# Row transposes of maxima and the masked sums issued as products of 32 columns, and placed behind the values of their step

## The chip, the cores and the metric

The kernel runs on one core of a Trainium2 chip. The metric is the device time of one execution in microseconds (us). Five engines take part, each with its own queue of instructions: TensorE (PE; its weight loads are listed apart as PEld), VectorE (DVE), ScalarE (ACT), GpSimd (POOL) and SyncE (SP), which issues most transfers. They meet through semaphores.

## The reference

One decoder layer over four sequences of 512 tokens with 512 features and 16 heads of 32. Biases, layer norms and the gate's softmax are as usual; cut to what matters:

```python
# self attention: causal softmax, masked scores are -inf
scores = jnp.where(causal, (q @ k.T) * SCALE, -jnp.inf)
x = x + softmax(scores) @ v @ o_w.T + o_b
# cross attention on ctx, without projections: masked scores are -10000, so in the first
# rows the masked keys can weigh as well
scores = jnp.where(causal, (qh @ kh.T) / sqrt(hd), -10000.0)
x = x + softmax(scores) @ vh
# feed forward: shared relu MLP, plus the expert output weighted by the top-2 gate
h = layernorm(x)
x = x + relu(h @ W_up.T) @ W_down.T + rw.sum() * (h @ W_expert)
```

## The kernel before

The work of a sequence (a "batch", 0 to 3) is laid out with features on the 128 partitions: four groups `g` of four heads of 32 features each, and 512 tokens along the free dimension, in four blocks of 128. Each attention has two passes.

`with_maxima` (line 905) computes scores with queries on partitions, and DVE takes the largest of each row. `split` (341) writes the negated maxima of a group as three bf16 parts into `parts[g % 2]`. `rows` (352) turns them on PE: four transposes of 128 by 128, one a token block, with `identb`, into a PSUM tile named `mt_...`, which is then copied to `mrow[g]`.

`attend` (954) computes the scores again with keys on partitions, in ten steps `n`. `scores` (393) makes the four heads' products with 32 rows of the array each (line 405) and adds the negated maxima as further products with `mrow[g]` (416). They fill two PSUM pairs, `sc_..._0` and `sc_..._1`, two heads in each. ACT takes the exponential of each pair (439), POOL zeroes the part above the diagonal (447), and `values`, called with two steps' delay, multiplies by the values (482), four heads side by side in 32 columns of the array each. The sums of exponentials are partly added up on DVE first (`add_up`, 547 to 552) and multiplied with ones afterwards (`summed`, 558).

In the cross attention masked keys can count, so there is more. `masked_sums` (371) spreads a group's maxima over its heads with one product of 128 columns by 512 (`same`, 374), `masked` (377) takes the exponential on ACT (381) as `ct_...`, and its closure `weigh` (385 to 389) is a memset and two multiplications of 128x512 on DVE. For groups 0 and 1 this is in the first pass; for groups 2 and 3 it is in `attend`. `divide(g)` (588) adds the weighted sums to the PSUM results and inverts the denominator: two additions that read `pv_...` from PSUM (592, 593), a 32x32 block transpose, a reciprocal and a transpose back (579, 581, 582). `scale` (571, 574) multiplies the group with it, on POOL for groups 0 to 2 and on DVE for group 3. For group 1 `divide` is called in the `values` of step 6; for groups 2 and 3, in the two `values` after the loop. `add_cross` (751) then transposes all four groups of the result, group by group, with PE (756).

PSUM holds four pairs of banks. The order on PE, DVE, ACT and POOL is the order in which the Python code issues (`manual_schedule`): each of these engines works through its queue as written, and an instruction that waits holds those behind it. The code that the change moves stands in the loop of `attend`:

```python
for n, pieces in enumerate(units):
    waiting.append(a.scores(pieces))
    if n in late:
        ...
        copies += a.rows(late[n], both)
        more = [a.masked_sums(2, both)] if two else []
        ...
    if a.cross and n == 7:
        todo.append(a.masked(*a.masked_sums(3)))
    if n in (4 if a.joined is None else 6, 6, 9) and todo:
        todo.pop(0)()
    if n in (3, 4) and put_off:
        put_off.pop(0)()
    if len(waiting) > 2:
        values()
```

`late` names the groups whose maxima are turned inside `attend`: groups 2 and 3 at step 3 of a self attention, group 3 at step 3 of the cross attentions 0 to 2, groups 2 and 3 at steps 3 and 5 of cross attention 3. `todo` holds the closures `weigh` of groups 2 and 3: they come at steps 6 and 9.

Of the kernel before, what the change touches and what calls it, by code (L numbers as in the profile page):

```python
# [18 lines left out]
P = 128  # L19
# [7 lines left out]
def decoder_layer(  # L27
# [21 lines left out]
    nc = tc.nc  # L49
    B, S, D = x.shape  # L50
    NH = 16
    HD = D // NH
    NT = S // P
    NC = D // P
    HG = P // HD
# [9 lines left out]
    def pair(name):  # L65

        return ps.tile([P, 2, S], F32, tag="ps", name=name)
# [65 lines left out]
    identb = const.tile([P, P], BF16, name="identb")  # L133
# [6 lines left out]
    same = const.tile([P, P], BF16, name="same")  # L140
# [34 lines left out]
    parts = []  # L175
# [90 lines left out]
    class Attention:  # L266
# [82 lines left out]
            nc.vector.tensor_copy(pt[:, :, :, 1], rest)  # L349
            nc.vector.tensor_tensor(pt[:, :, :, 2], rest, pt[:, :, :, 1], ALU.subtract)  # L350

        def rows(self, g, both=None, half=0):


            if both is None:
                tp = ps.tile([P, NT, P], BF16, tag="ps", name=f"mt_{self.name}_{g}")
            else:
                bank = both[:, 0, :].bitcast(BF16)
                tp = bank[:, half * S : (half + 1) * S].rearrange("p (i q) -> p i q", q=P)
            for i in range(NT):  # L360
                nc.tensor.transpose(tp[:, i, :], parts[g % 2][:, i, :], identb)
            self.mrow[g] = work.tile(
                [P, S], BF16, tag="mrow", name=f"mrow_{self.name}_{g}", bufs=4
            )

            def copy(engine=nc.vector.tensor_copy):
                engine(self.mrow[g], tp.rearrange("p i q -> p (i q)"))

            return [copy]

        def masked_sums(self, g, both=None):

            bc = (pair(f"mb_{self.name}_{g}") if both is None else both)[:, 1, :]
            nc.tensor.matmul(bc, lhsT=same, rhs=self.mrow[g], start=True, stop=True)
            return g, bc

        def masked(self, g, bc):
# [527 lines left out]
    def with_maxima(steps, a, first=0, norms=()):  # L905


        norms = list(norms)
        run(steps[:first])
        fill = matmuls(steps[first:])  # L910
        total = sum(1 if step.__name__ in ("share", "gate") else NC for step in steps[first:])

        units = []
        for g in range(0, NC, 2):
            units += [[(g, 1), (g + 1, 1)]]
            units += [u for k in (g, g + 1) for u in ([(k, 2), (k, 0)], [(k, NT - 1)])]

        lead = 2 if first else 0
        for _ in range(lead):
            next(fill)  # L920
        done, due, jobs, late = lead, float(lead), [], {3: NC - 1}
        todo = []
        for n, pieces in enumerate(units):
            new = a.maxima(pieces)
            if todo:
                todo.pop()(nc.gpsimd)
            if norms and n % 2 == 0:
                new.append(norms.pop(0))
            due += (total - lead) / len(units)

            count = round(due) - done
            for k in range(count):
                next(fill, None)
                done += 1
                if k == min(1, count - 1) and n in (5, 7):
                    jobs = a.rows((n - 5) // 2) + jobs
                if k == min(1, count - 1) and a.cross and n in (6, 8):
                    todo.append(a.masked(*a.masked_sums((n - 6) // 2)))
                if n == len(units) - 1 and k == count - (2 if count > 4 else 1):
                    if total >= 2 * len(units):  # L940
                        if a.cross:
                            a.rows(2)[0](nc.scalar.copy)
                    else:
                        late = {3: 2, 5: NC - 1}
                run(jobs[:1])
                jobs = jobs[1:]
            run(jobs)
            jobs = new
        for _ in fill:
            pass  # L950
        run(jobs)
        return late

    def attend(a, late):


        units = []
        for g in range(0, NC, 2):
            units += [[(g, 0)], [(g, 3), (g, 1)], [(g, 2), (g + 1, 2)]]
            units += [[(g + 1, 0)], [(g + 1, 3), (g + 1, 1)]]  # L960
        waiting, held, todo = [], [], []

        def values():
            made = waiting.pop(0)
            a.values(made)

            if len(made) > 1 and made[0][1] == 2:
                held.append(made[1:])
            elif waiting and waiting[0][0][1] > 0:
                if made[0][1] == 0 and held:  # L970
                    a.add_up(held.pop())
                a.add_up(waiting[0] if waiting[0][0][1] == 3 else waiting[0][:1])
                if waiting[0][0][1] == 2 and waiting[0][1][0] == a.joined:
                    a.join(waiting[0][1], waiting[1][0])

        for n, pieces in enumerate(units):
            waiting.append(a.scores(pieces))
            if n in late:
                two = a.cross and late[n] == NC - 1
                together = not a.cross and len(late) == 1  # L980
                both = pair(f"mt_{a.name}_both") if two or together else None
                copies = a.rows(2, both, 1) if together else []
                copies += a.rows(late[n], both)

                more = [a.masked_sums(2, both)] if two else []
                for copy in copies:
                    copy(nc.scalar.copy)
                todo.extend(a.masked(*each) for each in more)
            if a.cross and n == 7:
                todo.append(a.masked(*a.masked_sums(3)))  # L990
            if n in (4 if a.joined is None else 6, 6, 9) and todo:
                todo.pop(0)()
            if n in (3, 4) and put_off:
                put_off.pop(0)()
            if len(waiting) > 2:
                values()
        while waiting:
            values()

    with tc.manual_schedule(engines=BY_HAND):  # L1000
# [11 lines left out]
        for b in range(B):  # L1012
            more = b + 1 < B
# [4 lines left out]
            late = with_maxima(between_self, sa, skip, norms)  # L1018
            if b == B - 1:
                e.x = load_x(b)  # L1020
            attend(sa, late)
            if b > 0:
                add_bias(e)
# [8 lines left out]
            late = with_maxima(steps[3:], ca)  # L1032
            if b + 2 < B:
                after.x = load_x(b + 1)
            attend(ca, late)
            if more:
                cvs[b + 1] = load_cv(b + 1)
# [74 lines left out]
```

## Time and profile before

| | |
|---|---|
| median of 3 runs | 804.1 us (803.87 to 805.67) |
| span of the profiled execution | 803.7 us, 0.4 us under that median |
| mean granted TensorE clock | 0.998 |
| busy: PE, DVE, ACT, POOL | 794.0, 565.9, 395.2, 339.6 us |
| PE instructions (matrix products, weight loads) | 5588, 5592 |

A span runs from the first instruction to the last. Products on PE are pipelined: the profile's duration of one is longer than the time after which the next may start, so durations on PE overlap, and the times of start say more. A float32 product that is not a transpose stands in the trace as two records.

### The profile page before, as it was taken

What the parts mean: (1) busy time and instruction counts of PE and PEld (TensorE: products, weight loads), DVE (VectorE), ACT (ScalarE), POOL (GpSimd) and SP (SyncE); (2) the same over time, 40 slices, a digit from 0 to 9 for tenths busy, and PEclk for the clock granted to TensorE, in tenths of its full rate; (3) what the DMA queues carried; (4) which work ended last, traced back from release to release, by engine and by line L of the source; (5) the groups of instructions that cost most, each with busy time, mean ns of one, the idle gap of its engine ahead of it and who ended that gap; (6) DMA issues with size and microseconds to landing.
All of it is one profiled execution on the core that took longest, in us unless ns stands there. A gap on an engine that the chain in (4) does not pass through costs nothing.

```text
span 803.7 us, 13927 instructions
## 1 busy us (share of the span) xinstructions
PE 794.0 (99%) x5588; PEld 378.9 (47%) x5592; DVE 565.9 (70%) x963; ACT 395.2 (49%) x448; POOL 339.6 (42%) x523
## 2 busy tenths in 40 slices
PE   8999999999999999999999999999999999999998
PEld 6444454444444454444544455444444444444544
DVE  2378855889679854678867786588959766988512
ACT  2457516871456615567055742687156833674110
POOL 3434612564234732257332482256423652475100
PEclk9999999999999999999999999999999999999999
DMA  9710000001010000021100000000102000000101
GB/s 301 275 28 1 2 1 1 2 27 54 1 27 2 2 0 1 2 78 55 53 14 14 1 2 0 1 1 2 53 28 80 2 1 1 1 2 1 53 1 52
DMA packets 15282, 24.51 MB, mean 30 GB/s; under 512 B 2033, under 2 KB 5361, under 8 KB 15217
## 3 DMA queue, kind: packets, MB, share of 16 engines
q1 hardware_dynamic: 14496, 22.96, 8.6%
q8 instruction: 44, 0.72, 0.4%
q10 hardware_dynamic: 720, 0.66, 0.2%
q14 instruction: 22, 0.17, 0.1%
HBM read 19.42 MB, written 4.19 MB: 29 GB/s over the span
## 4 chain that ended last, share of the span: by engine, by line
PE 95%; ACT 2%; issue 1%; DMA 1%; DVE 0%; ACTq 0%
PE pm_qk L241 14%; PE pm_d L229 7%; PE pm_u L241 7%; PE pm_v L229 7%; PE pm_o L725 7%; PE pm_e L229 7%; PE pv_c L482 6%; PE pv_s L482 6%; PE sm_c L293 6%; PE sm_s L293 6%; PE sc_s L405 5%; PE sc_c L405 5%; PE sc_s L416 1%; PE sc_c L416 1%; PE tp_a L255 1%
## 5 line engine op out<-in xcount | busy, mean ns | idle before, releaser
L324 DVE TENSOR_REDUCE nm_s<-s_s 128x2 f32<-128x1024 f32 (+3 forms) x128 | 96.9, 810 | 34.7 <-POOL s_s L312 34.7
L324 DVE TENSOR_REDUCE nm_c<-s_c 128x2 f32<-128x1024 f32 (+3 forms) x128 | 95.8, 810 | 31.0 <-POOL s_c L312 31.0
L304 ACT COPY s_s<-sm_s 128x1024 f32<-128x1024 f32 x80 | 77.1, 1015 | 70.7 <-PE sm_s L293 36.7
L304 ACT COPY s_c<-sm_c 128x1024 f32<-128x1024 f32 x80 | 77.1, 1016 | 35.9 <-PE sm_c L293 16.2
L312 POOL TENSOR_SCALAR_AFFINE_SELECT s_c<-s_c 128x512 f32<-128x512 f32 (+1 forms) x80 | 43.9, 550 | 100.4 <-ACT s_c L304 100.4
L312 POOL TENSOR_SCALAR_AFFINE_SELECT s_s<-s_s 128x512 f32<-128x512 f32 (+1 forms) x80 | 43.8, 551 | 94.4 <-ACT s_s L304 94.4
L552 DVE TENSOR_TENSOR sum_s<-sum_s,pt_s 128x256 f32<-128x256 f32 (+2 forms) x72 | 59.9, 897 | 15.4 <-PE pv_s L482 15.4
L439 ACT ACTIVATE pt_c<-sc_c 128x1024 f32<-128x1024 f32 x64 | 61.7, 1031 | 18.1 <-PE sc_c L416 10.1
L447 POOL TENSOR_SCALAR_AFFINE_SELECT pt_c<-pt_c 128x512 f32<-128x512 f32 (+1 forms) x64 | 52.9, 833 | 20.7 <-ACT pt_c L439 20.2
L229 PE MATMUL pm_d<-wdown_sb,hT 128*128 128x512 f32 x128 | 61.5, 611 | 0.0
L241 PE MATMUL pm_qk<-xnT,wk_sb 128*128 128x512 f32 x128 | 61.0, 606 | 0.0
L241 PE MATMUL pm_u<-fT,wup_sb 128*128 128x512 f32 x128 | 59.3, 605 | 0.0
L439 ACT ACTIVATE pt_s<-sc_s 128x1024 f32<-128x1024 f32 x56 | 53.9, 1030 | 10.5 <-POOL pt_s L447 5.5
L229 PE MATMUL pm_v<-wv_sb,xnT 128*128 128x512 f32 x128 | 58.8, 600 | 0.0
L725 PE MATMUL pm_o<-wo_sb,oT_s 128*128 128x512 f32 x128 | 57.8, 596 | 0.0
L405 PE MATMUL sc_c<-cqT,ckT 32*128 32x384 f32 (+3 forms) x512 | 56.4, 464 | 0.9 <-ACT sum_c L439 0.9
L241 PE MATMUL pm_qk<-xnT,wq_sb 128*128 128x512 f32 x120 | 56.7, 605 | 0.0
L229 PE MATMUL pm_e<-wexp_sb,fT 128*128 128x512 f32 x120 | 56.3, 604 | 0.0
L447 POOL TENSOR_SCALAR_AFFINE_SELECT pt_s<-pt_s 128x512 f32<-128x512 f32 (+1 forms) x56 | 48.0, 865 | 16.9 <-ACT pt_s L439 16.2
L405 PE MATMUL sc_s<-qT,kT 32*128 32x128 f32 (+3 forms) x512 | 54.1, 464 | 0.9 <-ACT sum_s L439 0.9
L293 PE MATMUL sm_c<-ckT,cqT 32*128 32x512 f32 (+3 forms) x512 | 47.5, 460 | 0.0
L293 PE MATMUL sm_s<-kT,qT 32*128 32x512 f32 (+3 forms) x512 | 47.0, 461 | 0.0
(171 smaller groups left out, 1268.1 us busy)
## 6 DMA issues: line engine op xcount, KB each, us to landing
cv<-in_ctx_dram SPq DMA_DIRECT2D x16, 256.0 KB, 4.4
out_dram<-x SPq DMA_DIRECT2D x15, 256.0 KB, 2.0
xin<-in_x_dram SPq DMA_DIRECT2D x12, 256.0 KB, 2.8
x<-in_x_dram SPq DMA_DIRECT2D x12, 256.0 KB, 4.2
wq_sb<-in_wq_dram SPq DMA_DIRECT2D x2, 512.0 KB, 6.7
wk_sb<-in_wk_dram SPq DMA_DIRECT2D x2, 512.0 KB, 7.7
wv_sb<-in_wv_dram SPq DMA_DIRECT2D x1, 1024.0 KB, 7.8
wo_sb<-in_wo_dram SPq DMA_DIRECT2D x1, 1024.0 KB, 9.5
```

What stands on the lines that cost most here:

```text
L229: nc.tensor.matmul(pm, lhsT=lhs_t[:, c, t * P : (t + 1) * P], rhs=w[:, c, :], start=(c == 0), stop=(c == NC - 1),)
L241: nc.tensor.matmul(pm, lhsT=w[:, c, f * P : (f + 1) * P], rhs=rhs_t[:, c, :], start=(c == 0), stop=(c == NC - 1),)
L293: nc.tensor.matmul(scs[r // 2][:, r % 2, c : c + (i + 1) * P], lhsT=self.q_t[h, g, i * P : (i + 1) * P], rhs=self.k_t[h, g, : (i + 1) * P] ...
L304: nc.scalar.copy(s, scs[n])
L312: nc.gpsimd.affine_select(out=diagonal, in_=diagonal, compare_op=ALU.is_ge, fill=NEG, base=0, pattern=[[0, 2], [0, len(pieces)], [-1, P]], ...
L324: nc.vector.tensor_reduce(self.nm[g][:, i, 2 * n : 2 * n + 2], made[n][:, :, c : c + (i + 1) * P], axis=AX.X, op=ALU.max, negate=True,)
L405: nc.tensor.matmul(scs[r // 2][:, r % 2, c : c + S - j * P], lhsT=self.k_t[h, g, j * P : (j + 1) * P], rhs=self.q_t[h, g, j * P :], start= ...
L439: nc.scalar.activation(pt, scs[n], AF.Exp)
L447: nc.gpsimd.affine_select(out=diagonal, in_=diagonal, compare_op=ALU.is_ge, fill=0.0, base=0, pattern=[[0, 2], [0, len(pieces)], [1, P]], ...
L482: nc.tensor.matmul(pv[r * HD : (r + 1) * HD, u, j * P :], lhsT=ones if u else self.v[:, j, h * HD : (h + 1) * HD], rhs=pts[r // 2][:, r % ...
L552: nc.vector.tensor_tensor(to, to, pts[n][:, :, c : c + S - j * P], ALU.add)
L725: nc.tensor.matmul(pms[t // 2][:, t % 2, :], lhsT=a.out[:, c, t * P : (t + 1) * P], rhs=wo_sb[:, c, :], start=(c == 0), stop=(c == NC - 1),)
```

## The change

`rows` and `masked_sums` get an argument `columns`, which the calls in `attend` set. With it each transpose of 128 by 128 becomes four plain products, each with 32 columns of `parts` as its weights and `identb` as the moving operand, into 32 partitions of a float32 PSUM tile; the spreading product becomes four products of 32 columns. The calls in the first pass stay as they were. In the loop of `attend` the call of `values` moves from the end of a step to the place right behind `scores`.

```diff
-        def rows(self, g, both=None, half=0):
-            if both is None:
+        def rows(self, g, both=None, half=0, columns=False):
+            if columns:
+                tp = (pair(f"mt_{self.name}_{g}") if both is None else both)[:, half, :]
+                tp = tp.rearrange("p (i q) -> p i q", q=P)
+                for i in range(NT):
+                    for r in range(HG):
+                        nc.tensor.matmul(
+                            tp[r * HD : (r + 1) * HD, i, :],
+                            lhsT=parts[g % 2][:, i, r * HD : (r + 1) * HD],
+                            rhs=identb,
+                            start=True,
+                            stop=True,
+                        )
+            elif both is None:
...
-            for i in range(NT):
+            for i in range(NT if not columns else 0):
                 nc.tensor.transpose(tp[:, i, :], parts[g % 2][:, i, :], identb)
...
-        def masked_sums(self, g, both=None):
+        def masked_sums(self, g, both=None, columns=False):
...
-            nc.tensor.matmul(bc, lhsT=same, rhs=self.mrow[g], start=True, stop=True)
+            for r in range(HG if columns else 1):
+                h = slice(r * HD, (r + 1) * HD) if columns else slice(0, P)
+                nc.tensor.matmul(
+                    bc[h, :], lhsT=same[:, h], rhs=self.mrow[g], start=True, stop=True
+                )
...
             waiting.append(a.scores(pieces))
+            if len(waiting) > 2:
+                values()
             if n in late:
...
-                copies = a.rows(2, both, 1) if together else []
-                copies += a.rows(late[n], both)
-                more = [a.masked_sums(2, both)] if two else []
+                copies = a.rows(2, both, 1, columns=True) if together else []
+                copies += a.rows(late[n], both, columns=True)
+                more = [a.masked_sums(2, both, columns=True)] if two else []
...
-                todo.append(a.masked(*a.masked_sums(3)))
+                todo.append(a.masked(*a.masked_sums(3, columns=True)))
...
             if n in (3, 4) and put_off:
                 put_off.pop(0)()
-            if len(waiting) > 2:
-                values()
```

## The prediction

> **What bounds the kernel now.** I read the page first, then PE's timeline through the first cross attention (160 to 200 us), ACT's and DVE's timelines over the same stretch, and last what PE's weight loads waited for.
>
> ```profile
> PE 794.0 (99%) x5588; PEld 378.9 (47%) x5592; DVE 565.9 (70%) x963; ACT 395.2 (49%) x448; POOL 339.6 (42%) x523
> ...
> PE 95%; ACT 2%; issue 1%; DMA 1%; DVE 0%; ACTq 0%
> ```
>
> PE is busy all the time and is 95% of the chain that ended last. So PE time looks like the whole price. But a wait inside a block of merged products stays hidden in such a row. The timelines show two kinds of them. Columns: start, length, engine, line, operation, and in brackets idle time and what ended it.
>
> ```profile
> 164.88 0.40 PE L361 MATMUL mt_c_both<-identb,parts 128*128 128x128 bf16 x4
> 165.42 1.07 PE L482 MATMUL pv_c<-pt_c,cv 128*32 128x128 f32 x16
> 166.42 1.50 PE L405 MATMUL sc_c<-cqT,ckT 32*128 32x128 f32 x16
> ...
> 173.21 1.15 PE L405 MATMUL sc_c<-cqT,ckT 32*128 32x128 f32 x16
> ...
> 177.67 0.39 PE L374 MATMUL mb_c<-mrow_c,same 128*128 128x512 bf16 x1
> ...
> 178.99 1.53 PE L405 MATMUL sc_c<-cqT,ckT 32*128 32x512 f32 x6
> ...
> 186.46 1.04 PE L558 MATMUL pv_c<-sum_c,ones 128*32 128x512 f32 x8
> ...
> 192.70 2.07 PE L756 MATMUL tp_x<-ident,behT 128*128 128x128 f32 x16
> ```
>
> ```profile
> 164.79 1.94 ACT L439 ACTIVATE pt_c<-sc_c 128x1024 f32<-128x1024 f32 x2 [0.33 <-PE sc_c L416]
> ```
>
> First kind: the scores behind the transposes (166.42) take 1.50 us, the same products at 173.21 take 1.15. Their second pair of heads can't start before ACT has emptied the second pair of PSUM banks of the step before, and that exponential ends at 164.79 + 1.94 = 166.73. The second kind is DVE's.
>
> ```profile
> 172.97 0.06 DVE L387 MEMSET ct_c<- 128x1 f32 x1
> 173.07 0.69 DVE L388 TENSOR_TENSOR behT<-ct_c,behT 128x512 f32<-128x512 f32 x1
> 173.79 0.79 DVE L389 TENSOR_TENSOR ct_c<-ct_c,cnt 128x512 f32<-128x512 f32 x1
> 176.51 0.69 DVE L592 TENSOR_TENSOR ct_c<-pv_c,ct_c 128x512 f32<-128x512 f32 x1 [1.93 <-PE pv_c L482]
> ...
> 178.74 0.71 DVE L582 STREAM_TRANSPOSE dt_c<-rden_c 128x512 f32<-128x512 f32 x1
> 179.38 5.69 DVE L552 TENSOR_TENSOR sum_c<-sum_c,pt_c 128x256 f32<-128x256 f32 x6
> ...
> 185.12 0.98 DVE L388 TENSOR_TENSOR behT<-ct_c,behT 128x512 f32<-128x512 f32 x1
> 186.14 1.00 DVE L389 TENSOR_TENSOR ct_c<-ct_c,cnt 128x512 f32<-128x512 f32 x1
> 187.57 0.69 DVE L592 TENSOR_TENSOR ct_c<-pv_c,ct_c 128x512 f32<-128x512 f32 x1 [0.43 <-PE pv_c L558]
> ...
> 193.37 0.69 DVE L574 TENSOR_TENSOR behT<-behT,dt_c 128x512 f32<-128x512 f32 x1
> ```
>
> `weigh(2)` (172.97 to 174.58) fills a gap in which DVE would wait for PE until 176.51. From there to 194.06 DVE is busy but for 0.43 us. What ends this stretch, the scaling of group 3 (574), is the input of PE's last four transposes (756). The weight loads' timeline and the list of waits at line 756 show that PE waits for it already:
>
> ```profile
> 194.11 0.42 PEld L756 LDWEIGHTS tp_x<-ident,behT 128*128 128x128 f32 x4 [0.18 <-DVE behT L574]
> ```
>
> ```profile
>   DVE behT L574: 0.7, 4
> ```
>
> Four waits, one a batch. In the single records the 13th transpose starts 0.214 us behind the 12th instead of 0.109, so 0.105 us late. DVE's tail has no slack at all.
>
> **The change part by part.**
>
> *Array shape.* Before, PE goes scores (32 rows), transposes (128 by 128), values (32 columns), scores: three changes of shape. After it is two. In the single records a change costs 0.089 to 0.097 us beyond the time of the product ahead. There are 13 such places: 4 in the self attentions, 5 with transposes in the cross attentions, 4 spreading products at step 7. 13 x 0.095 = 1.24 us less PE work. Is it on the path? At 166.42 the second pair of heads starts at 166.79 in any case, ACT's end being set by the scores ahead of the moved part. That cover is 0.36 us here, 0.34 behind the transposes of self attention 0 (75.65, also 1.50 us long) and some 0.8 at step 7 (178.99 against 179.81, 1.53 us long). A saving of 0.095 vanishes in each. The one place where the records show no such wait is step 5 of batch 3. I count 0.1 us saved, with 1.24 as the bound if I misread the cover.
>
> *Thirty-two columns instead of 128.* A call of `rows` goes from 4 to 16 products, 13 calls, and 8 spreading products become 32: 180 more products and 180 more weight loads. A transpose starts 0.055 us after the one before, so a call takes 0.22. Four products in separate columns run side by side in the values (482): the records have the four 0.0066 us apart, and the next four 0.107 behind, which is what one float32 product of 128 elements takes alone. If the new ones do so too, a call still takes 4 x 0.055. Lower bound 0; if they ran one behind the other at 0.055, it is 13 x 12 x 0.055 = 8.6 us. I take 0, since the values have exactly this shape; up to 0.34 us a place would be covered as above.
>
> The Trainium skill ("TensorE: Matmul & The Clock Gate", section "Wait — 56ns, not 53.3ns?") speaks against the change here: products start no closer than about 25 ns, however small. By that rule a call would take 16 x 0.025 = 0.40 us, 0.18 more, 2.3 us in all, most of it under the same cover. The records' 0.0066 us within a group of four go against it, so the sum leaves it out.
>
> *Values earlier, transposes later.* ACT's copies to `mrow` come some 0.3 us later but run behind the same exponentials, and the next exponential had idled 0.29 us (168.09) or 0.34 (77.26) anyway; `mrow` is used two steps later. The order of instructions on ACT, POOL and SP is the same as before. I take 0. The float32 copy reads as many elements as the bf16 one (0.59 us).
>
> *`weigh(2)` moves.* DVE's order changes in one way, once in each cross attention: at step 6 `values` is now issued ahead of `weigh(2)`, so memset and two multiplications stand behind all five operations of `divide(1)`. `divide(1)` waits for PE until 176.51 as before, with DVE idle from 173.0, and `weigh(2)` runs at 179.38. Queued behind it on DVE are the six additions to `sum_c` (PE's line 558 waits for them), `weigh(3)`, both last divides and the scaling. It costs 174.58 - 172.97 = 1.61 us there. Off that goes the 0.43 idle before 187.57. Line 558 has slack: the additions end at 185.07, PE gets to it at 186.46. A delay of 1.61 uses that 1.39 up and makes PE 0.2 late there, which is part of its later wait and not on top of it. So the tail is 1.18 us later, and PE, which was already waiting, stands still for 1.18. Batches 1 and 2 have the same rows (idle 0.43 and 0.42): 1.18 and 1.19. Batch 3 has 0.37: 1.24. Sum 4.79.
>
> Bounds: beside POOL the same three operations took 2.13 us (`weigh(3)`, 185.01 to 187.14); moved at that price it is 1.7 a batch, 6.8 in all. Or `weigh(3)`, now 1.6 us later and past POOL's run of masks (182.57 to 186.6), shrinks to 1.61: then 0.66 a batch, 2.6 in all. I keep 1.18, since the two tend to cancel.
>
> Sum: 4.79 - 0.1 = 4.7 us on the profiled execution, 803.7 to 808.4; on the median, 804.1 to 808.8.
>
> **The rivals.** *Faster:* what decides is the PE time saved. It needs DVE's tail to be off the path, so that nothing but 13 x 0.095 counts: 804.1 - 1.2 = 802.9. For it: PE's 95% of the chain. Against it: the four waits for line 574.
>
> *No change:* the 1.61 us are absorbed by shorter operations on a quieter DVE, and the saving by ACT: 804.1. It needs DVE to win back 1.2 us over a stretch in which it is busy for 17 of 17.5 us.
>
> *Slower still:* the products of 32 columns don't overlap as the values do, and follow each other at 0.055 us. A call is 16 x 0.055 - 0.22 = 0.66 us longer. Four places have two calls, five have one, and each has 0.34 us of cover and the 0.095 saved: 4 x (1.32 - 0.44) + 5 x (0.66 - 0.44) = 4.6 us on top, 813.4. The shape of the values speaks against it.
>
> **How the numbers follow.** My case 0.82, slower still 0.08, no change 0.06, faster 0.04. A measurement of this kernel can tell about 0.2%, 1.6 us, from no change. The likeliest time is 808.8. The bounds of the moved multiplications give 806.6 (804.1 + 2.6 - 0.1) to 810.8; I end at 810.6, since both ends together are unlikely in all four batches, and leave the three rivals, 0.18, outside. Faster than 802.5: 0.03, most of the faster rival, whose 802.9 is no surer than a few tenths. Within 1.6 us: 0.07, no change and the rest of faster. Slower: 0.90.
>
> **What would show it.** In the profile after: on DVE the memset of `ct_c` at line 403 behind the second transpose of a divide, with the wait for `pv_c` in front of line 608 near 3.5 us; no or little idle time before the last but one divide; the list of waits at PE's transposes of `behT` showing DVE with some 5 us over four waits instead of 0.7; PE's busy time hardly changed. I am wrong if those waits stay at 0.7, if the self attentions get longer (then the new products cost PE time), or if the scores behind the moved products start their second pair later than before.

## The result, and the profile after

The changed kernel takes 807.2 us (median of 6 runs, 807.13 to 809.18) where the kernel before takes 804.0 (6 runs, 803.79 to 805.67): ratio 1.0038, 95% interval 1.0026 to 1.0049. The forecast was 808.8, within 806.6 to 810.6. It is slower, by 3.2 us instead of 4.7.

The two spans, 803.7 and 805.0, differ by less: in its first 20 us the profiled execution of before was granted a clock of 0.91 to 0.92 and that of after 1.00, and ACT's first write of `kT` starts at 19.06 us in the one and at 17.00 in the other. So traces are compared below from the start of that write to the start of ACT's last transfer of the output, which are the same instructions in each of them ("from `kT` on"): 781.99 us before, 785.41 after, 3.42 more.

The page of after, parts 1 and 4, first lines:

```profile
PE 795.5 (99%) x5772; PEld 380.3 (47%) x5772; DVE 564.9 (70%) x963; ACT 395.5 (49%) x448; POOL 332.2 (41%) x523
...
PE 89%; DVE 6%; issue 2%; ACT 2%; DMA 0%; ACTq 0%
```

Busy times have hardly moved; DVE's is a microsecond lower. But DVE, which had 0% of the chain that ended last, has 6% now. DVE's timeline in the first cross attention shows why (lines are 16 further down in this kernel; all times are some 2.06 us earlier than in the trace of before):

```profile
174.45 0.69 DVE L608 TENSOR_TENSOR ct_c<-pv_c,ct_c 128x512 f32<-128x512 f32 x1 [3.50 <-PE pv_c L498]
...
177.45 0.69 DVE L404 TENSOR_TENSOR behT<-ct_c,behT 128x512 f32<-128x512 f32 x1
178.18 1.00 DVE L405 TENSOR_TENSOR ct_c<-ct_c,cnt 128x512 f32<-128x512 f32 x1
179.11 5.65 DVE L568 TENSOR_TENSOR sum_c<-sum_c,pt_c 128x256 f32<-128x256 f32 x6
...
185.83 0.69 DVE L405 TENSOR_TENSOR ct_c<-ct_c,cnt 128x512 f32<-128x512 f32 x1
186.44 0.68 DVE L608 TENSOR_TENSOR ct_c<-pv_c,ct_c 128x512 f32<-128x512 f32 x1
...
192.23 0.69 DVE L590 TENSOR_TENSOR behT<-behT,dt_c 128x512 f32<-128x512 f32 x1
```

DVE waits 3.50 us for `divide(1)` with nothing to do, `weigh(2)` comes behind that, and from 174.45 to 192.92 there is no gap at all: 18.47 us where it was 17.55 (176.51 to 194.06), 0.92 more. PE loses this 0.92 in two places. The first is line 574 (558 before), the products of the summed exponentials with ones:

```profile
184.41 1.45 PE L574 MATMUL pv_c<-sum_c,ones 128*32 128x512 f32 x7
...
187.52 3.70 PE L229 MATMUL pm_v<-wv_sb,xnT 128*128 128x512 f32 x8
```

The block took 1.04 before. In the single records its third product now waits until 184.81 for the last of DVE's additions, and `pm_v` behind it starts 0.42 us later than before (187.52 + 2.06 = 189.58, against 189.16). The second place is PE's last four transposes. In the timeline of the weight loads and the list of waits, what was 0.18 of a wait (0.7 in four) is now 0.69, that is 0.51 more:

```profile
192.98 0.42 PEld L772 LDWEIGHTS tp_x<-ident,behT 128*128 128x128 f32 x4 [0.69 <-DVE behT L590]
```

```profile
  DVE behT L590: 4.5, 8
```

(8 counts PE and its weight loads, for four places; the weight loads alone have 2.7 of the 4.5, and the 0.7 of before was theirs alone.) Matched by ACT's instructions, which stand in the same order in both kernels, after falls behind by 0.92 us at the end of each of the four cross attentions and gains 0.28 at step 5 of batch 3. But for the two instructions of ACT that read the moved products at that step itself, the distance changes nowhere else by more than 0.1.

The new products, in PE's timeline of after, self attention 0 and cross attention 0:

```profile
72.92 0.63 PE L360 MATMUL mt_s_both<-identb,parts 128*32 128x128 bf16 x32
73.48 1.60 PE L421 MATMUL sc_s<-qT,kT 32*128 32x128 f32 x16
...
163.71 0.41 PE L360 MATMUL mt_c_both<-identb,parts 128*32 128x128 bf16 x16
163.93 0.40 PE L388 MATMUL mt_c_both<-mrow_c,same 128*32 128x512 bf16 x4
164.26 1.61 PE L421 MATMUL sc_c<-cqT,ckT 32*128 32x128 f32 x16
```

32 products take 73.48 - 72.92 = 0.56 us with one change of shape (0.096) in it: 0.0145 each, four in 0.058. And the scores behind them got longer, 1.60 and 1.61 us instead of 1.50: what PE saved ahead of them it now waits inside them. In the single records of cross attention 0 their second pair of heads starts at 164.73 us, which is the 166.79 of before less 2.06.

### The profile page after: what moved, and what is told of

Its sections match the earlier page's. It is cut to its first block, busy times and chain, and to the rows that moved or that the text cites. A ratio compares the mean times of both kernels' runs of the same rounds, so it can differ in the third digit from the quotient of the medians.

```text
span 805.0 us, 14291 instructions
## 1 busy us (share of the span) xinstructions
PE 795.5 (99%) x5772; PEld 380.3 (47%) x5772; DVE 564.9 (70%) x963; ACT 395.5 (49%) x448; POOL 332.2 (41%) x523
## 4 chain that ended last, share of the span: by engine, by line
PE 89%; DVE 6%; issue 2%; ACT 2%; DMA 0%; ACTq 0%
PE pm_qk L241 14%; PE pm_d L229 7%; PE pm_u L241 7%; PE pm_o L741 7%; PE pm_e L229 6%; PE pv_s L498 6%; PE pm_v L229 6%; PE sm_c L293 6%; PE sm_s L293 5%; PE sc_s L421 5%; PE sc_c L421 5%; PE pv_c L498 3%; DVE sum_c L568 2%; PE sc_s L432 1%; PE sc_c L432 1%
## 5 line engine op out<-in xcount | busy, mean ns | idle before, releaser
L463 POOL TENSOR_SCALAR_AFFINE_SELECT pt_c<-pt_c 128x512 f32<-128x512 f32 (+1 forms) x64 | 48.7, 763 | 30.7 <-ACT pt_c L455 30.1
```

Of the source, the lines that this page charges most:

```text
L463: nc.gpsimd.affine_select(out=diagonal, in_=diagonal, compare_op=ALU.is_ge, fill=0.0, base=0, pattern=[[0, 2], [0, len(pieces)], [1, P]], ...
```

## The experiments

The theory: all of the loss is `weigh(2)` standing behind the wait of `divide(1)`, which makes DVE's tail of each cross attention later, and PE with it. The main rival: the products of 32 columns, or the later copies, cost time themselves. "From `kT` on" is against the 781.99 us of before.

### Put `weigh` back ahead of the values (e1_weigh_first)

```diff
+            if n in (4 if a.joined is None else 6, 6, 9) and todo:
+                todo.pop(0)()
             if len(waiting) > 2:
                 values()
...
-            if n in (4 if a.joined is None else 6, 6, 9) and todo:
-                todo.pop(0)()
```

> The changed kernel with one thing put back: weigh is issued ahead of values again, so that DVE's order is that of before; the products of 32 columns and the moved values stay. Theory (DVE's tail pays for all of it): the 0.92 us a batch are gone, and only the saved change of shape at step 5 of batch 3 is left, some 0.1 to 0.25 us: ratio 0.9995 to 1.000, about 803.8 where before takes 804.0; the waits of PE's last four transposes of behT back at 0.7 us in all. Rival (the products of 32 columns, or the later copies to mrow, cost time): it stays near the changed kernel, ratio 1.003 to 1.004.

Measured: ratio 0.9993 (0.9985 to 1.0002), 803.6 us; from `kT` on, 0.26 less than before. The list of waits at the transposes of the result is that of before again:

```profile
  DVE behT L590: 0.7, 4
```

So the two lines of code hold the whole loss. (They also move the call for `weigh(3)` at step 9, but among DVE's instructions `weigh(3)` stands at the same place in the traces of before and after, between the additions and `divide(2)`.) The 0.26 us are all at step 5 of batch 3, more than the 0.1 I had counted. PE's timeline there, before and in this kernel:

```profile
720.67 0.39 PE L416 MATMUL sc_c<-mrow_c,onesb 32*128 32x512 bf16 x4
721.17 0.40 PE L361 MATMUL mt_c_both<-identb,parts 128*128 128x128 bf16 x4
...
723.57 1.15 PE L405 MATMUL sc_c<-cqT,ckT 32*128 32x128 f32 x16
```

```profile
718.74 0.39 PE L432 MATMUL sc_c<-mrow_c,onesb 32*128 32x512 bf16 x4
...
721.36 1.15 PE L421 MATMUL sc_c<-cqT,ckT 32*128 32x128 f32 x16
```

2.90 us between the two rows before, 2.62 here. The first transpose of before starts 0.174 us later than a change of shape explains, and the list of PE's weight-load waits has one wait at line 361 for DVE's line 593: the PSUM pair was still being read by `divide(0)`. Behind the values it is free. 0.174 + 0.095 = 0.27.

### The kernel before, with `weigh` behind the values (e2_weigh_late)

```diff
-            if n in (4 if a.joined is None else 6, 6, 9) and todo:
-                todo.pop(0)()
             if n in (3, 4) and put_off:
                 put_off.pop(0)()
             if len(waiting) > 2:
                 values()
+            if n in (4 if a.joined is None else 6, 6, 9) and todo:
+                todo.pop(0)()
```

> The kernel before with one thing changed: weigh is issued behind values; transposes of 128 by 128 ahead of the values, as before. Theory: the whole loss without any of the new products, 4 x 0.92 = 3.7 us, ratio 1.0045, about 807.7, a little above the changed kernel, which had the saving at step 5 of batch 3. Rival (the new products are to blame): within 0.3 us of before, ratio 1.000.

Measured: ratio 1.0044 (1.0031 to 1.0057), 807.8 us; from `kT` on, 3.71 more. The list of waits at the transposes of the result:

```profile
  DVE behT L574: 4.5, 8
```

The loss is there without a single new product, in the size expected. With the run above the rival has fallen from both sides.

### The products alone (e3_columns_only)

```diff
             waiting.append(a.scores(pieces))
-            if len(waiting) > 2:
-                values()
             if n in late:
...
             if n in (3, 4) and put_off:
                 put_off.pop(0)()
+            if len(waiting) > 2:
+                values()
```

(against the changed kernel: its products of 32 columns stay, `values` goes back to the end of the step.)

> The changed kernel with values put back to the end of the step: only the shape of the products is changed, and they stand between scores and values. DVE's order is that of before. Theory: one change of shape less at 13 places is hidden by ACT at 12 of them, ratio 0.9995 to 1.000, about 803.8. Rival (PE's time counts, as its 95% of the chain suggests): 13 x 0.095 = 1.2 us faster, ratio 0.9985, about 802.8. A second rival (products of 32 columns follow each other instead of running side by side): 0.66 us a call more, beyond the cover, 1 us or more slower.

Measured: ratio 0.9996 (0.9987 to 1.0005), 803.9 us; from `kT` on, 0.11 less. One change of shape is saved at 13 places, 1.24 us of PE time in all (13 x 0.095), and one of them, 0.095, arrives. The other twelve end in the wait for ACT inside the next scores.

### The moved order alone (e6_full_moved)

```diff
-                copies += a.rows(late[n], both, columns=True)
+                copies += a.rows(late[n], both)
...
-                todo.append(a.masked(*a.masked_sums(3, columns=True)))
+                todo.append(a.masked(*a.masked_sums(3)))
```

(against the first experiment; the other two calls likewise.)

> e1_weigh_first with the products put back to 128 columns: values moved ahead, weigh ahead of values, transposes of 128 by 128 and one spreading product, as in before, behind the values. The number of shape changes is that of before, one more than in e1_weigh_first at 13 places. Theory: no difference from before or from e1_weigh_first but step 5 of batch 3, where the wait of 0.17 us for the PSUM tile should be gone with the move and the 0.095 stay: 0.1 to 0.2 us under before, 0.1 above e1_weigh_first. Rival (shape changes count): 1.2 us slower than e1_weigh_first.

Measured: ratio 0.9998 (0.9989 to 1.0006), 804.3 us beside 804.55 for before in that comparison; from `kT` on, 0.15 less than before, and 0.11 more than the first experiment. Move and shape add up: 0.15 + 0.11 = 0.26, both at the one place without cover.

### Each new product twice (e5_twice)

```diff
-                for i in range(NT):
+                for i in [i for i in range(NT) for _ in range(2)]:
                     for r in range(HG):
```

> e1_weigh_first with every product of 32 columns in rows issued twice, one token block after the other, same result: PE gets 13 x 0.22 = 2.9 us more work. Theory (12 of the 13 places stand ahead of a wait for ACT's exponential): in the self attentions 0.44 us more against a cover of 0.34 + 0.095, in the cross attentions 0.22 against 0.36 + 0.095; only step 5 of batch 3 has none. So 0.2 to 0.4 us slower than e1_weigh_first, about 803.9 where that took 803.64. Rival (PE's time is the price): 2.9 us slower than e1_weigh_first, 806.5.

Measured: ratio 0.9998 (0.9990 to 1.0007), 804.4 us beside 804.55; from `kT` on, 0.21 more than before, 0.47 more than the first experiment, a little over what I expected, and far from 2.9. Of the 0.47, matched by ACT's instructions, about 0.25 come in the four self attentions and 0.22 at step 5 of batch 3. PE's timeline in self attention 0:

```profile
73.57 1.08 PE L360 MATMUL mt_s_both<-identb,parts 128*32 128x128 bf16 x64
74.58 1.15 PE L421 MATMUL sc_s<-qT,kT 32*128 32x128 f32 x16
```

64 products take 1.01 us, a change of shape among it, and the scores behind them are down from 1.60 to 1.15, their length without a wait. So the cover is real, about 0.45 us here, and now used up.

### `weigh(2)` on POOL (e4_weigh_pool)

```diff
-                todo.pop(0)()
+                todo.pop(0)(nc.gpsimd if n == 6 else nc.vector)
```

> The changed kernel with weigh(2) on POOL instead of DVE, issued at the same place, behind values. POOL's own masks then stand behind some 2.6 us of multiplications. Theory (what counts is DVE's time between divide(1) and the scaling of group 3, not the order as such): the 1.76 us leave DVE, ratio 0.9995 to 1.001, about 804.0, unless the two multiplications on POOL hold up the masks that ACT's next exponentials and the values need, of which POOL's gaps of 0.8 to 1.6 us at this place leave little. Rival (the order itself, or the products): ratio stays at 1.003 to 1.004.

Measured: ratio 1.0025 (1.0012 to 1.0037), 806.6 us; from `kT` on, 2.83 more. The main expectation failed and its exception came true. Timelines of POOL, and of PE in the same stretch:

```profile
176.16 1.28 POOL L404 TENSOR_TENSOR behT<-ct_c,behT 128x512 f32<-128x512 f32 x1
177.52 1.26 POOL L405 TENSOR_TENSOR ct_c<-ct_c,cnt 128x512 f32<-128x512 f32 x1
...
182.22 4.05 POOL L463 TENSOR_SCALAR_AFFINE_SELECT pt_c<-pt_c 128x256 f32<-128x256 f32 x4
```

```profile
183.48 1.38 PE L498 MATMUL pv_c<-pt_c,cv 128*32 128x512 f32 x6
```

The waits for DVE's last scaling are back at 0.7 us, so DVE's tail is no later than PE any more. But PE itself is: POOL's run of masks starts 0.92 us later than before (182.22 against 182.57, in a trace that is 1.27 ahead), and the values of group 3 are broken up, 1.38 us for six records where eight took 1.04; in the single records the third starts at 184.24, 0.04 after the end of the mask that it waits for. 0.75 to 0.79 us a batch go there instead. That POOL's masks are the whole reason is argued from these rows, not tried apart.

### One more multiplication on DVE (e8_one_more)

```diff
             if len(waiting) > 2:
                 values()
+            if a.cross and n == 6:
+                nc.vector.tensor_tensor(scratch, cnt, cnt, ALU.mult)
```

(in the kernel before; nobody reads `scratch`.)

> The kernel before with one multiplication of 128x512 more on DVE in each cross attention, into a scratch tile that nobody reads, behind values of step 6, where the changed kernel has weigh(2). It measures the price of DVE time there. Theory: 0.69 us alone, up to 1.0 beside POOL, less the 0.43 us in which DVE idled before divide(2), four times: 1.0 to 2.3 us slower, about 805.6. Rival (the order counts, or any DVE work is hidden): nothing, 804.1. Rival (no slack at all): 4 x 0.69 = 2.8 us or more.

Measured: ratio 1.0015 (1.0005 to 1.0025), 805.7 us beside 804.55; from `kT` on, 1.00 more, 0.25 a batch. That is the lower end of what I expected. In its trace the extra multiplication takes 0.72 us, 0.64 from start to start, and the gap of 0.43 before `divide(2)` is gone. But other lengths change with it: the six additions take 0.43 more (6.06 instead of 5.63) and `weigh(3)` 0.40 less (1.73 instead of 2.13). 0.64 - 0.43 + 0.43 - 0.40 = 0.24, near the 0.25. The price of DVE time at this place comes to its length less that gap, because the other two changes nearly cancel.

### A faster version (e7_sum_first)

The first experiment, and the product of the summed exponentials of group 2 with ones moved ahead of the ones-products of group 3, by 0.86 us:

```diff
             for u in range(1 if g in self.added else 2):
+                if u and self.cross and js == {0} and g == NC - 1:
+                    self.summed(g - 1, self.pv[g - 1])
...
-                    self.summed(g - 1, self.pv[g - 1])
+                    if g != NC - 1:
+                        self.summed(g - 1, self.pv[g - 1])
                     self.divide(g - 1)
```

> A try at a faster kernel: e1_weigh_first, and in the first values after the loop of a cross attention the product of sum_c with ones for group 2 stands ahead of the ones-products of group 3 instead of behind them, 0.86 us earlier on PE, so that DVE's divide(2) no longer waits for it (0.43 us) and the tail ends earlier. Theory: PE's four waits of 0.105 us for the scaling of group 3 go, 0.4 us; about 803.2, unless the additions to sum_c come too late for the earlier place (they end at 185.07, PE would be there at 185.60). Rival (the tail isn't what these four waits are from): as e1_weigh_first.

Measured: ratio 0.9988 (0.9979 to 0.9998), 803.7 us beside 804.55; from `kT` on, 0.92 less than before and 0.65 less than the first experiment. PE's timeline:

```profile
192.97 1.91 PE L775 MATMUL tp_x<-ident,behT 128*128 128x128 f32 x16
194.72 2.74 PE L229 MATMUL pm_v<-wv_sb,xnT 128*128 128x512 f32 x6
```

The wait is gone: 1.75 us from the first transpose to the next product, 1.91 (192.70 to 194.61) before. That is 0.16 a batch, the 0.105 that I had read and 0.05 more. It is faster than both kernels, than the one before by about a thousandth.

## Why the prediction was right, point by point

**The mechanism held.** DVE's order was the step that decided, with the sign, the place and the wait in front of `divide(1)` as forecast (near 3.5 us, measured 3.50). Where PE would pay was forecast less well. I had put it 0.2 us late at line 558, as part of its later wait and not on top of it, and looked for some 5 us of waits at the last transposes. It was 0.42 late there in each batch and 0.51 at the transposes, where the weight loads' waits come to 2.7 us in all. It was a part and not on top: 0.42 + 0.51 is DVE's 0.92 but for rounding.

**The mis-sized term is `weigh(2)` in the sum, 1.18 us a batch against 0.92.** I took the moved operations at 1.61 and `weigh(3)` as unchanged at 2.13, since "the two tend to cancel". They didn't quite. Measured from start to start: `weigh(2)` 1.76 (177.35 to 179.11), 0.15 more; `weigh(3)` 1.74 (184.70 to 186.44) instead of 2.13, 0.39 less, as POOL's run of masks was over by then (its last one ends at 185.26) and line 405, from 185.83 on, took 0.69 instead of 1.00; the additions 5.59 instead of 5.63; `divide(1)` 0.03 more. 1.18 + 0.15 - 0.39 - 0.04 + 0.03 = 0.93. Over the four batches that is 4.79 - 3.68 = 1.1 of the 1.5 us by which the forecast missed; 0.2 more are at step 5 of batch 3 (below), and the last 0.2 lie between the traces' 3.42 and the medians' 3.2. My lower bound had named the effect and I should have gone towards it.

**The saved changes of shape: hidden at 12 of 13 places, as forecast**; shown by the products alone (0.11 of 1.24) and by doubling them. At step 5 of batch 3 I counted 0.1 and it was 0.26 to 0.28: I overlooked that the transposes of before waited there for their PSUM pair.

**Thirty-two columns: no cost, as taken.** The records are 0.0145 us apart on average and four fit into the time of one product. The Trainium skill's floor of about 25 ns from start to start ("TensorE: Matmul & The Clock Gate", section "Wait — 56ns, not 53.3ns?") would make it, as an estimate, 0.40 us for 16; the trace has 0.22 (163.71 to 163.93). In this trace it does not hold for products in four column groups.

**The rivals.** Faster needed DVE's tail off the path; it is on it. No change needed DVE to win back 1.2 us; it won back 0.3. Slower still needed products one behind the other; they overlap.

## What to carry to other kernels

When a call is moved in a program whose queues run as written, list what it issues on every engine, not only the one that it is moved for: here `values` carried a DVE operation that waits past one that could have run. Work that fills a wait is free only where it stands; put behind the wait it costs about its length less the next gap, and less or more by what the operations behind it change (here 1.76 - 0.43 = 1.33 by that rule, and 0.92 measured, with `weigh(3)` 0.39 shorter). A saving on an engine that is 99% busy is worth nothing where the next block on it waits inside for another engine, and such a wait shows as one block being longer than the same block elsewhere.

## What I had not expected

The same multiplication of 128x512 on DVE takes 0.69 us or 1.00. It took 0.69 wherever POOL ran nothing beside it, and each of the long ones stood beside a mask or a multiplication of POOL, though some that overlapped a mask in part were short as well; no run varied POOL alone. So an operation that is moved can change the length of others (`weigh(3)`, 2.13 to 1.74). Three operations moved from DVE to POOL cost nearly as much there (2.83 us against 3.42), by way, as argued above, of masks that came 0.92 us late.
